# A fused two-layer latent-attention kernel: averages in two PSUM banks a step apart, apart-row scores and small values by chunk of two batches, GpSimd's ones and products later and a step apart

## The chip, the cores and the metric

The kernel runs on one core of one Trainium2 chip. The metric is device time in microseconds of one launch; the profile is one such execution. The engines are TensorE (PE, with its weight loads shown as PEld), VectorE (DVE), ScalarE (ACT), GpSimd (POOL) and the queue of SyncE (SP), which issues the DMAs. Each engine works through its own instructions in order.

## The reference

16 batches of 64 latents of width 128 pass through two layers. Each layer is cross attention to a context, then a scan over the latents, then a feed-forward part, each on the layer-normed latents and added to them:

```python
x = x + _L0_xattn_ref(ctx_1024, _layernorm(x), ...)     # 16 heads of 64
x = x + _L0_attn_ref(_layernorm(x), ...)                # selective scan
x = x + _L0_ffn_ref(_layernorm(x), ...)                 # small attention, then 8 experts, top 2, and a shared one
x = x + _L1_xattn_ref(ctx_1024, _layernorm(x), mask, ...)
x = x + _L1_attn_ref(_layernorm(x), ...)                # convolution and a scan in blocks
x = x + _L1_ffn_ref(_layernorm(x), ...)                 # weights and inputs rounded to 4 bits
...
# cross attention, both layers (layer 1 with a mask over the context rows):
kv_input = concatenate([layernorm(ctx), layernorm(latents)])   # 1601 + 64 rows
logits = einsum('bhld,bhsd->bhls', q * scale, k * scale)
out = einsum('bhls,bhsd->bhld', softmax(logits), v) @ Wo
```

Everything is float32.

## The kernel before

**Tiling.** The cross attention is done for groups: a group is a layer, a batch and half of its 16 heads, 8 heads x 64 latents = 512 columns, so there are 64 groups. The query weights are folded with the key weights (`wqk`) and the value weights with the output weights (`wvo`), so that keys and values are the normed context itself. `kv` holds a batch's 13 tiles of 128 rows (12 context tiles `G`, and a last one with 64 context rows and the 64 latent rows), with a column of ones as the 129th for the softmax's denominator; `kvT` is its transpose. The 1601st context row doesn't fit and is handled apart: its scores `se` (`apart_scores`, L403 to L418) are small matmuls of the latents `xnT` with a folded vector per head (`ge`), and its contribution comes in as `xeb` times `ee` when the averages are read.

**Steps.** `run` counts steps `n`; 13 steps (`NT`) are a group's score tiles. `step` issues at each `n`:

- `scores` (L643): one matmul of 512 columns (L656) into one of three PSUM tiles `s`; DVE keeps the running maximum over the tiles, `R` (L664 masked, layer 1; L666 layer 0), and ACT copies the tile to `st` in SBUF (L669, L671). `st` tiles hold two score tiles each, and there are 11 of them.
- `average` (L709), `LAG` = 21 steps behind the scores: four matmuls of 129 columns (L719), `st` as weights and `kv` as the moving side, accumulated over the 13 tiles in `av`, one PSUM tile that spans two banks. At a group's first tile nothing is issued; the first two tiles come together a step later. So with i = n mod 13 the averages of step i = 7 are the last of a group, step 8 has none, step 9 has eight matmuls.
- `gather` (L721): after the last average DVE reads `av` with four operations (L728) into `aq`. Only then may the next group's averages start, since there is one `av`.
- after a group's scores: `maximum` (transposes `tm`, L680, and the row's maximum, with `se`), `spread` (`mb`, L698), and at every second step `weigh`: DVE subtracts the maximum (L706), ACT takes the exponential (L707).
- after its averages: `denominator` (reciprocal L767, division on GpSimd L768), `turn` (transposes `at`, L779), and for the second half of every second batch `output` (L791), at fixed offsets of steps.

The preparation of a batch runs beside it: `context_load` (L468) at 48 steps ahead issues on SP the DMAs of `kv` (L486, L487 from the context in layer 0; L489, L490 from the stored normed copy in layer 1), and on GpSimd a memset of the ones column (L472). Three `kv` tiles rotate, so both wait for the last average of three batches earlier. `context` (L576), a generator that gives one portion of work per step, norms it (layer 0: first reduction L606 on DVE, statistics on ACT, L612, square root on GpSimd, L135), transposes it, stores it and calls `with_latents` (L563), which multiplies `kv` by the norm's weight on GpSimd (four operations, L570) and adds the latents' columns and rows. The scan and feed-forward parts of finished batches (`scan0`, `moe`, `scan1`, `ffn`) are generators too, from which a budget takes portions between the steps. In `moe` the values `mv` (L943) of the small attention are one matmul per batch.

**Order.** The Tile framework's scheduler orders each engine's instructions from these issues; `behind` adds order-only dependencies that keep a portion of side work behind the main instruction just issued. So the order on an engine may differ from the order of issue in small ways.

```python
LAG = 21
...
self.pss = pool("pss", 3, space=PSUM)      # s
self.psa = pool("psa", 1, space=PSUM)      # av
self.pst = pool("pst", 3, space=PSUM)      # everything else, "tp"
...
grp["av"] = self.psa.tile([P, 2, NQ], F32, tag="av", name=f"av{g}")
```

Of the kernel before, what the change touches and what calls it, by code (L numbers as in the profile page):

```python
# [79 lines left out]
class Kernel:  # L80
# [236 lines left out]
    def raw_pair(self, lay, l, r, g, queue):  # L317


        if lay == 0:  # L320
            t = self.at.tile([P, 2, NQ], F32, tag="st2", name=f"raw{l}{g}", bufs=11)
            pair = [t[:, i, :2 * D].rearrange("p (m d) -> p m d", m=2) for i in range(2)]
        else:
            pair = [self.at.tile([P, 2, D], F32, tag="raw", name=f"raw{n}{g}", bufs=3) for n in (l, r)]
        for t, n in zip(pair, (l, r)):
            queue.dma_start(out=t, in_=self.a[f"L{lay}{n}"].rearrange("(m p) d -> p m d", p=P)[:, 2 * g:2 * g + 2, :])
        return pair
# [75 lines left out]
    def apart_scores(self, lay, b):  # L403

        nc = self.nc
        bl = b % BG
        xnT = self.lat_of[lay, b // BG][0][:, bl * L:(bl + 1) * L]
        t = self.tp(f"se{lay}_{b}")
        ge = self.ge[:, b, :].rearrange("p (n i) -> p i n", i=2)
        for i in range(2):  # L410
            nc.tensor.matmul(t[i * L:(i + 1) * L, :H // 2], xnT, ge[:, i, :], start=True, stop=True)
        se = self.sm([P, H // 2], "se")
        if lay == 0:
            nc.vector.tensor_copy(se, t[:, :H // 2])
        else:
            nc.vector.tensor_scalar(se, t[:, :H // 2], self.mex[:, b:b + 1], None, ALU.add)
        self.se_of[lay, b] = se
        yield 0.3  # L418
# [49 lines left out]
    def context_load(self, lay, b):  # L468
        nc = self.nc
        kv = self.at.tile([P, G + 1, D + 1], F32, tag="kv", name=f"kv{lay}_{b}", bufs=3)  # L470
        kvT = self.at.tile([P, SK + L], F32, tag="kvT", name=f"kvT{lay}_{b}", bufs=2)
        nc.gpsimd.memset(kv[:, :, D:], 1.0)  # L472
        if lay == 0:
            ctxd = self.a["ctx"]
            tiles = ctxd[b, :P * G, :].rearrange("(p g) d -> p g d", g=G)
            nc.gpsimd.memset(kv[64:P, G, :D], 0.0)
            if b == 0:

                self.raw_kv = [self.at.tile([P, 2, NQ], F32, tag="st2", name=f"rkv{j}", bufs=11).rearrange("p i (g d) -> p (i g) d", d=D) for j in range(2)]
                for lo in range(0, G, 4):  # L480
                    nc.sync.dma_start(out=self.raw_kv[lo // 8][:, lo % 8:lo % 8 + 4, :], in_=tiles[:, lo:lo + 4, :])
                    if lo == 0:
                        self.raw0.append(self.raw_pair(0, "WqT", "WkT", 1, nc.sync))
                nc.sync.dma_start(out=self.raw_kv[1][:REM, G - 8, :], in_=ctxd[b, P * G:SK, :])
            else:
                nc.sync.dma_start(out=kv[:, :G, :D], in_=tiles)  # L486
                nc.sync.dma_start(out=kv[:REM, G, :D], in_=ctxd[b, P * G:SK, :])  # L487
        else:
            nc.sync.dma_start(out=kv[:, :, :D], in_=self.xh[b])  # L489
            nc.sync.dma_start(out=kvT[:, :SK], in_=self.xhT[b])  # L490
        self.kv_of[lay, b] = (kv, kvT)

    def first_context(self):
# [28 lines left out]
        def turned(lo, hi):  # L522
# [7 lines left out]
            raw = self.at.tile([P, 2, NQ], F32, tag="st2", name=f"xt{lo}", bufs=11)[:, 0, :w]  # L530
# [29 lines left out]
        self.with_latents(0, 0)  # L560
        yield 0.0

    def with_latents(self, lay, b):  # L563
# [3 lines left out]
        kv, kvT = self.kv_of[lay, b]  # L567

        for lo, hi in ((0, 4), (4, 7), (7, 10), (10, G + 1)):
            nc.gpsimd.tensor_tensor(kv[:, lo:hi, :D], kv[:, lo:hi, :D], self.row(self.vec[:, w1, :], [P, hi - lo, D]), ALU.mult)  # L570
        xnT, xn = self.lat_of[lay, b // BG]
        bl = b % BG
        nc.scalar.activation(kvT[:, SK:], xnT[:, bl * L:(bl + 1) * L], AF.Identity, bias=self.nvcol[:, b1:b1 + 1])
        nc.sync.dma_start(out=kv[REM:, G, :D], in_=xn[(bl % 2) * L:(bl % 2 + 1) * L, bl // 2, :])

    def context(self, lay, b):  # L576
# [26 lines left out]
        elif lay == 0:  # L603
            nmean, rstd, v, off = (self.sm([P, n], f"c{x}") for x in ("mean", "rstd", "var", "off"))
# [35 lines left out]
        self.with_latents(lay, b)  # L640
        yield 1.0

    def scores(self, g, i):  # L643
# [6 lines left out]
        if i % 2 == 0:  # L650
            n = min(2, NT - i)
            grp["st"].append(self.at.tile([P, n, NQ], F32, tag=f"st{n}", name=f"st{g}_{i // 2}", bufs=11 if n == 2 else 2))
# [56 lines left out]
    def average(self, g, i):  # L709
# [4 lines left out]
        if i == 0:  # L714
            grp["av"] = self.psa.tile([P, 2, NQ], F32, tag="av", name=f"av{g}")
        for k in range(4):
            o = grp["av"][:, k // 2, k % 2 * (D + 1):(k % 2 + 1) * (D + 1)]
            st = grp["st"][i // 2][:, i % 2, k * P:(k + 1) * P]
            nc.tensor.matmul(o, st, self.kv_of[lay, b][0][:, i, :], start=(i == 0 and k % 2 == 0), stop=(i == NT - 1 and k % 2 == 1))  # L719

    def gather(self, g):  # L721

        nc, grp = self.nc, self.groups[g]
        aq = grp["aq"] = self.at.tile([P, 4, D + 1], F32, tag="aq", name=f"aq{g}", bufs=2)
        xeb = self.xeb_of[grp["key"][:2]]
        for k in range(4):
            o = grp["av"][:, k // 2, k % 2 * (D + 1):(k % 2 + 1) * (D + 1)]
            nc.vector.scalar_tensor_tensor(aq[:, k, :], xeb, grp["ee"][:, k:k + 1], o, ALU.mult, ALU.add)  # L728
        for k in ("st", "R", "av", "mb"):
            grp.pop(k)  # L730

    def finish(self, g):
# [6 lines left out]
        xeb, av = self.xeb_of[lay, b], grp["av"]  # L739
        blocks = av[:, :, :2 * (D + 1)].rearrange("p k (j d) -> p k j d", j=2)  # L740
        four = lambda v: v.rearrange("p (k j) -> p k j", k=2)
        den, rd = self.sm([P, 4], "den"), self.sm([P, 4], "rd")
        nc.vector.tensor_tensor(four(den), blocks[:, :, :, D], four(grp["ee"]), ALU.add)
        nc.vector.reciprocal(rd, den)
        turned = []
        for k in range(4):
            nc.vector.scalar_tensor_tensor(aq[:, k, :D], xeb[:, :D], grp["ee"][:, k:k + 1], blocks[:, k // 2, k % 2, :D], ALU.mult, ALU.add)
# [13 lines left out]
        for k in ("st", "R", "av", "mb"):  # L761
            grp.pop(k)
# [147 lines left out]
    def moe(self, gr):  # L910
        nc, tc, a = self.nc, self.tc, self.a
        X = self.X[:, gr * CG:(gr + 1) * CG, :]
        with tc.tile_pool(name="mo1", bufs=1) as one, tc.tile_pool(name="mo2", bufs=2) as work:
# [28 lines left out]
            for b in range(BG):  # L942
                nc.tensor.matmul(t[b % 2 * L:(b % 2 + 1) * L, b // 2 * 32:(b // 2 + 1) * 32], xT[:, b * L:(b + 1) * L], fWkvT[:, 32:], start=True, stop=True)  # L943
# [475 lines left out]
    def run(self, out):  # L1419
# [6 lines left out]
        done = lambda lay, b: start(lay, b) + LAG + 9  # L1426
# [12 lines left out]
        for lay in range(2):  # L1439
# [14 lines left out]
            for b in range(NB):  # L1454
                if lay or b:
                    prep.append((max(start(lay, b) - (28 if lay == 0 else 12), 3), 2 if lay == 0 else 1, self.context(lay, b)))
                prep.append((start(lay, b) - 2 if lay or b else 12, 1, self.apart_scores(lay, b)))
# [10 lines left out]
        self.summed, self.upto_sums = False, upto_sums  # L1468
# [93 lines left out]
    def step(self, n, ng):  # L1562
# [4 lines left out]
        ga, ia = divmod(n - LAG, NT)  # L1567
        if 0 <= ga < ng and ia:
            if ia == 1:
                self.average(ga, 0)  # L1570
            self.average(ga, ia)
            if ia == NT - 1:
                if ga == ng - 1:
                    self.upto_sums()
                    self.finish(ga)
                else:
                    self.gather(ga)
# [15 lines left out]
        if 0 <= d < ng:  # L1593
# [3 lines left out]
            with self.behind():  # L1597
                if o == 0:
                    self.denominator(d)
                elif o == 4:  # L1600
                    self.turn(d)
                if o == 7 and b % 2 and half:
                    self.output(lay, b // 2)
                elif o == 9 and d == ng - 2:
# [58 lines left out]
```

## Time and profile before

| what | value |
|---|---|
| median of 3 runs | 1988.09 us (1985.63 to 1988.84) |
| the profiled execution, its own time | 1984.66 us |
| its span, first to last instruction | 1983.0 us |
| granted TensorE clock over the span | 0.999 |
| PE busy | 1938.7 us |
| DVE busy | 1557.6 us |
| ACT busy | 1380.2 us |
| POOL busy | 516.1 us |

Busy time is the time in which at least one instruction of an engine was running. In the profile a line such as L719 is a line of the kernel's file; "x6656" is the number of records, and one float32 matmul of the program shows as two records. In the groups, the number after the bar is busy time in us, then the mean of one record in ns, then the idle time of the engine just before these instructions and what ended it. In the waits, a row is: engine and instruction that waited, what it waited for, us in total, how many times, the longest. In the timeline a row is: start in us, length, engine, line, instruction, how many merged.

### The profile page before, as it was taken

Reading aid. Unit: us, or ns where it says so; the run is one execution under the profiler, and the core shown is the slowest. Engines: PE = TensorE matmul, PEld = TensorE weight load, DVE = VectorE, ACT = ScalarE, POOL = GpSimd, SP = SyncE. Lnnn points to the kernel's source line nnn. Section 1 sums busy time; section 2 is a strip of 40 time slices with the busy share of each in tenths; the row PEclk is TensorE's granted clock in tenths of the full one; section 3 lists DMA queues with packets and bytes.
Section 4 is the critical chain, followed back from the end, with each engine's and each line's share of the span. In section 5 each row is a group of like instructions: output and inputs, shape, how many; then the busy total and the mean of one; then the engine's idle time right before and its main releaser. Section 6 shows DMA issues by size and latency. Waiting matters only on the chain. (4 is left out here: it accounts for less than half of the span.)

```text
span 1983.0 us, 32835 instructions
## 1 busy us (share of the span) xinstructions
PE 1938.7 (98%) x12083; PEld 1476.6 (74%) x12083; DVE 1557.6 (79%) x2976; ACT 1380.2 (70%) x2642; POOL 516.1 (26%) x579
## 2 busy tenths in 40 slices
PE   8999999999999999999999999999999999999998
PEld 5777777677777767768777777777778777787787
DVE  6977667977868787775998778898786878777885
ACT  5787778887768888656766667776665656765561
POOL 5211122543113552121542202442110121101000
PEclk9999999999999999999999999999999999999999
DMA  6121112322122121221221112221120211101000
GB/s 178 51 68 43 46 53 77 92 58 70 29 81 85 60 82 53 66 79 45 68 82 53 41 32 71 70 58 53 49 67 2 58 37 37 42 17 37 24 1 22
DMA packets 144110, 110.82 MB, mean 56 GB/s; under 512 B 13762, under 2 KB 130254, under 8 KB 143950
## 3 DMA queue, kind: packets, MB, share of 16 engines
q1 hardware_dynamic: 143406, 108.46, 18.8%
q8 instruction: 96, 1.57, 0.3%
q14 instruction: 64, 0.52, 0.1%
q10 hardware_dynamic: 544, 0.26, 0.0%
HBM read 80.23 MB, written 27.41 MB: 54 GB/s over the span
## 5 line engine op out<-in xcount | busy, mean ns | idle before, releaser
L719 PEld LDWEIGHTS av<-kv,st 128*128 128x128 f32 x6656 | 853.3, 192 | 324.0 <-issue 305.9
L719 PE MATMUL av<-kv,st 128*128 128x129 f32 x6656 | 866.3, 275 | 3.2 <-DVE aq L728 2.5
L656 PE MATMUL s<-qT,kvT 128*128 128x512 f32 x1664 | 850.6, 599 | 16.0 <-ACT st L671 8.7
L707 ACT ACTIVATE st<-st 128x1024 f32<-128x1024 f32 (+1 forms) x448 | 445.6, 999 | 113.2 <-DVE st L706 110.4
L706 DVE TENSOR_TENSOR st<-st,mb 128x1024 f32<-128x1024 f32 (+1 forms) x448 | 505.2, 1133 | 19.8 <-PE mb L698 19.8
L669 ACT ACTIVATE st<-s,mcol 128x512 f32<-128x512 f32 x416 | 283.8, 683 | 217.3 <-DVE R L664 173.5
L671 ACT COPY st<-s 128x512 f32<-128x512 f32 x416 | 240.5, 580 | 132.5 <-DVE R L666 101.1
L656 PEld LDWEIGHTS s<-qT,kvT 128*128 128x128 f32 x1664 | 258.7, 191 | 77.9 <-ACT st L671 28.3
L664 DVE SCALAR_TENSOR_TENSOR R<-s,mcol,R 128x512 f32<-128x512 f32 x352 | 261.8, 744 | 42.3 <-PE s L656 40.8
L666 DVE TENSOR_TENSOR R<-s,R 128x512 f32<-128x512 f32 x352 | 240.5, 683 | 44.4 <-PE s L656 43.7
L570 POOL TENSOR_TENSOR kv<-kv,vec 128x384 f32<-128x384 f32 (+1 forms) x128 | 132.2, 1054 | 169.3 <-DMA xh<-kv 63.9
L768 POOL TENSOR_TENSOR aq<-aq,rd 128x512 f32<-128x512 f32 x63 | 71.4, 1134 | 354.6 <-DVE rd L767 349.3
L872 POOL TENSOR_TENSOR db<-sc_u,bb 128x512 f32<-128x512 f32 x64 | 84.6, 1324 | 141.0 <-DVE h L883 86.1
L889 POOL TENSOR_TENSOR sc_y<-sc_y,h 128x512 f32<-128x512 f32 x60 | 86.0, 1434 | 98.1 <-DVE h L888 81.5
L883 DVE TENSOR_TENSOR_SCAN h<-da,db 128x512 f32<-128x512 f32 x64 | 82.3, 1286 | 0.0
L621 ACT ACTIVATE kv<-kv,coff,crstd 128x128 f32<-128x128 f32 x182 | 76.3, 492 | 4.1 <-POOL coff L618 4.1
L612 ACT ACTIVATE scr<-kv,cmean 128x128 f32<-128x128 f32 x182 | 73.0, 401 | 3.0
L666 DVE TENSOR_TENSOR R<-s,st 128x512 f32<-128x512 f32 x32 | 22.0, 687 | 66.7 <-PE s L656 54.6
L135 POOL TENSOR_TENSOR crstd<-cvar,neghalf 128x13 f32<-128x13 f32 x14 | 34.2, 2440 | 152.0 <-DVE cvar L616 152.0
L728 DVE SCALAR_TENSOR_TENSOR aq<-xeb,ee,av 128x129 f32<-128x129 f32 x252 | 72.0, 341 | 1.0 <-PE av L719 0.8
L455 PE MATMUL q<-xnT,wqk 128*128 128x128 f32 x512 | 69.5, 278 | 0.3
L455 PEld LDWEIGHTS q<-xnT,wqk 128*128 128x128 f32 x512 | 63.1, 192 | 8.5 <-issue 3.0
(409 smaller groups left out, 1927.8 us busy)
## 6 DMA issues: line engine op xcount, KB each, us to landing
bb<-bcd SPq DMA_DIRECT2D x64, 256.0 KB, 4.6
xh<-kv SPq DMA_DIRECT2D x16, 832.0 KB, 4.8
kv<-xh SPq DMA_DIRECT2D x16, 832.0 KB, 5.6
kvT<-xhT SPq DMA_DIRECT2D x16, 800.0 KB, 4.6
xhT<-kvT SPq DMA_DIRECT2D x15, 800.0 KB, 3.4
kv<-in_ctx_dram SPq DMA_DIRECT2D x15, 768.0 KB, 5.5
ew<-in_e1T_dram SPq DMA_DIRECT2D x36, 64.0 KB, 1.8
ew<-in_e3T_dram SPq DMA_DIRECT2D x36, 64.0 KB, 1.9
```

Source lines behind the costliest of these rows:

```text
L455: nc.tensor.matmul(t[:, k * P:(k + 1) * P], self.wqk[:, g * 4 + k, :], xnT, start=True, stop=True)
L570: nc.gpsimd.tensor_tensor(kv[:, lo:hi, :D], kv[:, lo:hi, :D], self.row(self.vec[:, w1, :], [P, hi - lo, D]), ALU.mult)
L656: mm = nc.tensor.matmul(s, self.kv_of[lay, b][1][:, i * P:(i + 1) * P], q, start=True, stop=True)
L664: mx = nc.vector.scalar_tensor_tensor(R, s, mc, last, ALU.add, ALU.max)
L666: mx = nc.vector.tensor_tensor(R, s, last, ALU.max)
L669: ev = nc.scalar.activation(st, s, AF.Identity, bias=mc)
L671: ev = nc.scalar.copy(st, s)
L706: nc.vector.tensor_tensor(st, st, self.row(mb, [P, n, NQ]), ALU.subtract)
L707: nc.scalar.activation(st, st, AF.Exp)
L719: nc.tensor.matmul(o, st, self.kv_of[lay, b][0][:, i, :], start=(i == 0 and k % 2 == 0), stop=(i == NT - 1 and k % 2 == 1))
L872: nc.gpsimd.tensor_tensor(db, u, self.row(bb[:, 0, s % 2, :], both), ALU.mult)
L889: nc.gpsimd.tensor_tensor(y, y, h, ALU.add)
```

## The change

- **Averages.** `av` becomes two PSUM tiles of one bank each, `av0` and `av1`, with two of the four blocks each. `step` issues the first half's matmuls 21 steps behind the scores and the second half's 22 steps behind; at the very last tile both come in one step. Each half is read by two DVE operations after its own last average. `denominator`, `turn` and `output` come one step later, as does the start of the scan parts (`done`). There are 12 `st` tiles of two in place of 11.
- **Apart-row scores.** One matmul for a chunk of two batches (128 latents, 2 x 16 columns), called for every second batch, in place of two matmuls of 64 latents and 8 columns for each batch. Half of its output is not used (each batch's latents with the other batch's vector). DVE copies four blocks of 64 x 8 per chunk to the two `se` tiles, and in layer 1 adds the mask with an operation for each.
- **Small values.** `mv` in `moe` is a matmul per chunk of 128 latents in place of one per batch of 64.
- **GpSimd.** The memset of the ones, except for the first two batches of layer 0, moves from `context_load` to `with_latents`, after the latents' columns on ACT; the zeroing of the last tile's lower half in layer 0 moves from `context_load` to the beginning of `context`. The four products with the norm's weight are issued one step apart instead of all in one step.

```diff
-    def apart_scores(self, lay, b):
+    def apart_scores(self, lay, c):
...
-        xnT = self.lat_of[lay, b // BG][0][:, bl * L:(bl + 1) * L]
-        t = self.tp(f"se{lay}_{b}")
-        ge = self.ge[:, b, :].rearrange("p (n i) -> p i n", i=2)
-        for i in range(2):
-            nc.tensor.matmul(t[i * L:(i + 1) * L, :H // 2], xnT, ge[:, i, :], start=True, stop=True)
-        se = self.sm([P, H // 2], "se")
-        if lay == 0:
-            nc.vector.tensor_copy(se, t[:, :H // 2])
-        else:
-            nc.vector.tensor_scalar(se, t[:, :H // 2], self.mex[:, b:b + 1], None, ALU.add)
-        self.se_of[lay, b] = se
+        xnT = self.lat_of[lay, c // CG][0][:, (c % CG) * P:(c % CG + 1) * P]
+        t = self.tp(f"se{lay}_{c}")
+        nc.tensor.matmul(t[:, :2 * H], xnT, self.ge[:, 2 * c:2 * c + 2, :].rearrange("p b h -> p (b h)"), start=True, stop=True)
+        for j in range(2):
+            se = self.sm([P, H // 2], "se")
+            mine = t[j * L:(j + 1) * L, j * H:(j + 1) * H].rearrange("p (n i) -> p i n", i=2)
+            for i in range(2):
+                nc.vector.tensor_copy(se[i * L:(i + 1) * L, :], mine[:, i])
+            if lay:
+                nc.vector.tensor_scalar(se, se, self.mex[:, 2 * c + j:2 * c + j + 1], None, ALU.add)
+            self.se_of[lay, 2 * c + j] = se
...
# context_load
-        nc.gpsimd.memset(kv[:, :, D:], 1.0)
+        if lay == 0 and b < 2:
+            nc.gpsimd.memset(kv[:, :, D:], 1.0)
+            nc.gpsimd.memset(kv[64:P, G, :D], 0.0)
...
-            nc.gpsimd.memset(kv[64:P, G, :D], 0.0)
...
# with_latents, now a generator
-        for lo, hi in ((0, 4), (4, 7), (7, 10), (10, G + 1)):
-            nc.gpsimd.tensor_tensor(kv[:, lo:hi, :D], kv[:, lo:hi, :D], self.row(self.vec[:, w1, :], [P, hi - lo, D]), ALU.mult)
         xnT, xn = self.lat_of[lay, b // BG]
         bl = b % BG
         nc.scalar.activation(kvT[:, SK:], xnT[:, bl * L:(bl + 1) * L], AF.Identity, bias=self.nvcol[:, b1:b1 + 1])
+        if lay or b > 1:
+            nc.gpsimd.memset(kv[:, :, D:], 1.0)
+
+        for lo, hi in ((0, 4), (4, 7), (7, 10), (10, G + 1)):
+            nc.gpsimd.tensor_tensor(kv[:, lo:hi, :D], kv[:, lo:hi, :D], self.row(self.vec[:, w1, :], [P, hi - lo, D]), ALU.mult)
+            yield 0.6
         nc.sync.dma_start(out=kv[REM:, G, :D], in_=xn[(bl % 2) * L:(bl % 2 + 1) * L, bl // 2, :])
...
# context, layer 0, before the first reduction
+            nc.gpsimd.memset(kv[64:P, G, :D], 0.0)
...
-    def average(self, g, i):
+    def average(self, g, i, j):
...
         if i == 0:
-            grp["av"] = self.psa.tile([P, 2, NQ], F32, tag="av", name=f"av{g}")
-        for k in range(4):
-            o = grp["av"][:, k // 2, k % 2 * (D + 1):(k % 2 + 1) * (D + 1)]
-            st = grp["st"][i // 2][:, i % 2, k * P:(k + 1) * P]
-            nc.tensor.matmul(o, st, self.kv_of[lay, b][0][:, i, :], start=(i == 0 and k % 2 == 0), stop=(i == NT - 1 and k % 2 == 1))
+            t = self.psa.tile([P, NQ], F32, tag=f"av{j}", name=f"av{g}_{j}")
+            grp["av", j] = t[:, :2 * (D + 1)].rearrange("p (k d) -> p k d", k=2)
+        for k in range(2):
+            st = grp["st"][i // 2][:, i % 2, (2 * j + k) * P:(2 * j + k + 1) * P]
+            nc.tensor.matmul(grp["av", j][:, k, :], st, self.kv_of[lay, b][0][:, i, :], start=(i == 0 and k == 0), stop=(i == NT - 1 and k == 1))
...
# moe
-            for b in range(BG):
-                nc.tensor.matmul(t[b % 2 * L:(b % 2 + 1) * L, b // 2 * 32:(b // 2 + 1) * 32], xT[:, b * L:(b + 1) * L], fWkvT[:, 32:], start=True, stop=True)
+            for c in range(CG):
+                nc.tensor.matmul(t[:, c * 32:(c + 1) * 32], xT[:, c * P:(c + 1) * P], fWkvT[:, 32:], start=True, stop=True)
...
# run
-        done = lambda lay, b: start(lay, b) + LAG + 9
+        done = lambda lay, b: start(lay, b) + LAG + 10
...
# step
-        ga, ia = divmod(n - LAG, NT)
-        if 0 <= ga < ng and ia:
+        for j in range(2):
+            ga, ia = divmod(n - LAG - j, NT)
+            if not 0 <= ga < ng or not ia:
+                continue
+            end = ga == ng - 1 and ia == NT - 1
+            if j and end:
+                continue
             if ia == 1:
-                self.average(ga, 0)
-            self.average(ga, ia)
-            if ia == NT - 1:
-                if ga == ng - 1:
-                    self.upto_sums()
-                    self.finish(ga)
-                else:
-                    self.gather(ga)
+                self.average(ga, 0, j)
+            self.average(ga, ia, j)
+            if end:
+                self.late_half = ga
+            elif ia == NT - 1:
+                self.gather(ga, j)
+        if self.late_half is not None:
+            self.average(self.late_half, NT - 1, 1)
+            self.upto_sums()
+            self.finish(self.late_half)
+            self.late_half = None
...
-                if o == 0:
+                if o == 1:
                     self.denominator(d)
-                elif o == 4:
+                elif o == 5:
                     self.turn(d)
-                if o == 7 and b % 2 and half:
+                if o == 8 and b % 2 and half:
                     self.output(lay, b // 2)
```

## The prediction

> **What bounds the kernel now.** I read the page first (busy shares and groups), then the waits of PE, then PE's timeline at two kinds of place, and last the waits of POOL and of the context's first reduction on DVE.
>
> The page:
>
> ```profile
> PE 1938.7 (98%) x12083; PEld 1476.6 (74%) x12083; DVE 1557.6 (79%) x2976; ACT 1380.2 (70%) x2642; POOL 516.1 (26%) x579
> ...
> L719 PE MATMUL av<-kv,st 128*128 128x129 f32 x6656 | 866.3, 275 | 3.2 <-DVE aq L728 2.5
> L656 PE MATMUL s<-qT,kvT 128*128 128x512 f32 x1664 | 850.6, 599 | 16.0 <-ACT st L671 8.7
> ```
>
> PE is the bound. The program has 3328 average matmuls and the profile 6656 records, so each matmul is two records. A change can gain here in two ways only: fewer or cheaper PE instructions, or fewer stalls of PE. The page's idle time, 1983.0 - 1938.7 = 44 us, is too small a measure of stalls: a matmul's modelled end reaches into the gap after it. I therefore use the distance from start to start. PE's timeline, a group end of layer 1:
>
> ```profile
> 1214.02 1.02 PE L656 MATMUL s<-qT,kvT 128*128 128x512 f32 x2
> 1214.88 1.05 PE L719 MATMUL av<-kv,st 128*128 128x129 f32 x8
> 1215.77 1.88 PE L656 MATMUL s<-qT,kvT 128*128 128x512 f32 x4
> 1219.51 1.12 PE L656 MATMUL s<-qT,kvT 128*128 128x512 f32 x2 [1.86 <-ACT st L669]
> 1220.47 2.84 PE L719 MATMUL av<-kv,st 128*128 128x129 f32 x24
> ```
>
> One score tile takes 0.86 us (1214.02 to 1214.88), one tile's averages 0.89 us (to 1215.77); a step is 1.75 us and 832 of them are 1456 us of the span. But at a group's end three score tiles stand in a row (x4 and x2, no averages between), because step 8 has no averages and step 9's are behind a scheduler that put tile 10 first. The third should start at 1215.77 + 2 x 0.86 = 1217.49 and starts at 1219.51: 2.02 us lost, for a PSUM tile that ACT had not yet read. In the instruction order 31 of 64 ends have tiles 8, 9, 10 in a row, 30 others 8 and 9. Measured start to start over all group ends: tile 9 is late 15 times, tile 10 15 times, the new group's first average 14 times (it waits for the four readings of the one `av` tile, L728), in sum 25.7 us. A middle tile (0 to 8, 12) is late by about 1 us in all 64 groups together.
>
> The second place, the apart-row scores:
>
> ```profile
> 508.45 1.05 PE L719 MATMUL av<-kv,st 128*128 128x129 f32 x8
> 509.43 0.29 PE L411 MATMUL se<-ge,xnT 128*64 128x8 f32 x4
> 509.65 1.13 PE L656 MATMUL s<-qT,kvT 128*128 128x512 f32 x2
> 510.62 1.05 PE L719 MATMUL av<-kv,st 128*128 128x129 f32 x8
> ```
>
> From av to s is 1.20 us where 0.89 is usual, from s to av 0.97 where 0.86 is usual: 0.31 + 0.11 = 0.42 us for four tiny records. The pattern is the same at nearly all 32 calls.
>
> **The change, part by part.** (a) Apart scores by chunk. Removed: 32 calls x 0.415 us (the trace's ns at this place) = 13.3 us. Added: 16 calls of one 128x32 matmul, two records, on the whole array. The nearest row is the router's, small but untiled:
>
> ```profile
> 1408.93 1.05 PE L719 MATMUL av<-kv,st 128*128 128x129 f32 x8
> 1409.82 0.51 PE L1055 MATMUL router<-w_WrT,mo_xT 128*128 128x8 f32 x4
> 1410.19 1.10 PE L656 MATMUL s<-qT,kvT 128*128 128x512 f32 x2
> 1411.13 1.05 PE L719 MATMUL av<-kv,st 128*128 128x129 f32 x8
> ```
>
> Here four records cost (1410.19 - 1409.82) + (0.94 - 0.86) = 0.45 us, 0.112 each. Two are 0.224 us, 16 calls 3.6 us. Gain 9.7 us. Here a rule speaks for the old form: the Trainium skill, "TensorEngine Tiling (Array Packing)", section Overview, gives narrow operands up to 2x when the array is split, two tiles side by side. The trace shows that overlap (the second record of a pair starts 7 ns after the first), and by this rule alone a call would be two pairs of 0.112, 7.2 us in all, and the gain only 3.6. But the measured call has 93 ns ahead of the tiny records and some 310 to the next start. The page has the reason too (section Tiling Modes, key properties: changing the mode drains TensorE), without a price; the row has it. I take 9.7, and 3.6 as the low end. Beside it DVE gets 64 copies and 16 additions in place of 32 operations: copies of 8 columns have a row at 156 ns (L414), the old masked form 215 (L416), so 64 x 0.156 + 16 x 0.2 = 13 us in place of 5.9, +7 us on an engine with 425 us free. It is hidden as long as three score tiles in PSUM bridge it: one call is 0.6 us in layer 0 and about 0.85 in layer 1, against 1.75 - 1.35 = 0.4 us free on DVE in each step (0.74 for the maximum and half of 1.21 for the weighing), so the backlog is gone in one or two steps. I charge 1 us in all, 0 to 5.
>
> (b) Small values by chunk: 4 calls of 8 tiled records, about 0.55 us each without their wait, become 4 untiled records at 0.112, 0.45. Gain 0.4 us; 0.45 and 0.87 us of waits for ACT ahead of two of them stay.
>
> (c) Averages in two halves a step apart. The number of matmuls and records is the same. The order of instructions of the changed kernel reads, between tiles 7 and 12: tile 8, 2 averages, tile 9, 4, tile 10, 6, tile 11, 4; 51 of the 64 ends have exactly this and only two still have 9 and 10 side by side. So tile 9 starts half of 0.89 = 0.45 us later by work instead of waiting, and tile 10 another 0.89, 1.34 together. I let each stall of the trace shrink by that (tile 9 by 0.45, tile 10 of a row of three by 1.34, the first average by 0.9, as its two readings now have two score tiles and a half step of averages in front of them), and count 0.10 us for a refill where something is left: of 25.7 us, 20.0 go. The big ones remain in part (the 2.02 us above keeps 0.7: DVE and ACT are also held by scan work there). Against it: new small stalls at two boundaries in place of one, 3 us by the rate of middle tiles (two or three tiles at 1 us per 64). Net 17 us; at most 25.7, at least 6 if DVE and ACT are the ones that can't keep up and the wait only moves. Alternating between two banks is no new cost: the old order already changed banks after every second matmul, and x8 still took 0.89.
>
> Moved with it by one step: the division (L767, L768), the turn, the output. PE then has turn at step 0 instead of after tile 12, and the output beside `mb` at step 3; these are PE work, no wait: the division has four steps (7 us) as before for 1.13 us on POOL. The `st` tiles live a step longer, and one buffer more (two steps) covers it; ACT's waits for a free one (6.4 + 1.3 us) can only shrink. The kv tile comes free a step later, see the rival. In the tail one reading fewer stands before the last group's averages (0.5 us gained), one `den` operation of 0.16 us is added: +0.3.
>
> (d) GpSimd.
>
> ```profile
> POOL kv L472 <- PE av L719: 184.7, 22, 30.8
> ...
> PE at L779 <- POOL aq L768: 2.4, 1, 2.4
> ```
>
> The memset of ones waited 184.7 us at the head of POOL's queue; moved, it waits for nothing. But PE waited for POOL only once, 2.4 us. DVE's waits for POOL's square roots (L135) are 16 us in all, the longest 2.4, and DVE has the slack. Gain 0 to 3, I take 0.5. The products, a step apart, end three steps later, still more than 20 steps ahead of the first average that reads them; behind them on SP only the latents' rows. The zeroing of the last tile's lower half now stands directly before DVE's second reduction of the same tile; POOL must be less than a step late there. I charge 1 us, 0 to 4.
>
> Sum: 9.7 + 0.4 + 17 + 0.3 + 0.5 - 1 - 1 = 25.9, say 26 us. The profiled run took 1984.66 us (span 1983.0), so it becomes 1958.7; the median of three is 1988.09, 3.4 above the profiled run, so 1962.
>
> **The rivals.** *The stalls only move* (chance 0.2). DVE at 79% and ACT at 70% are the reason that a PSUM tile is late; if their backlog at a group end is the whole matter, (c) gives 6 instead of 17, (a) its 9.7 less 3 for the bunched copies: 12 us, 1976. For it: ACT's 173.5 us of waits for DVE's maximum. Against: DVE itself waits 170 us for PE's scores, so it is ahead on average.
>
> *A late context, slower than before* (0.07). The kv tile is free only after the second half's last average, 1.75 us later; its load is waiting for that, and DVE's reduction heads DVE's queue:
>
> ```profile
> DVE cmean L606 <- DMA kv<-in_ctx_dram: 10.4, 9, 2.1
> ```
>
> With 1.75 us more at 13 contexts of layer 0 that is up to 10.4 + 13 x 1.75 = 33 us of DVE held, the maximum behind it, the PSUM tile behind that. If PE took all of it, 33 - 26 = 7 us slower, 1995; it decides from about 26 of the 33 us reaching PE, 2 us per context. Against: none of the nine waits of before (up to 2.1 us) is followed by a stall of PE, three tiles last 5 us, and in the new order this reduction stands behind tile 10's maximum in 13 of 14 cases (7 of 14 before), which gives the step back.
>
> *It does not do what it says*, no change (0.05): the scores' gain is eaten by copies and the stalls come back elsewhere. The order of instructions speaks against it.
>
> **How the numbers follow.** My forecast, 0.68: 1962, its own range 1952 to 1970. Best case: 25.7 + 9.7 + 3 = 38 us, 1950. Down the stalls that only move, 1976, with 4 more for the ends of (a) and (d), 1980. The range 1950 to 1980 leaves out the late context, the no change and a little on the fast side. A measurement of this kernel tells about 0.2%, 4 us, from no change. Faster by more: 0.68 + 0.2 less 0.01; within: 0.05; slower: 0.08.
>
> **What would show it.** Right: no x4 of s at group ends in PE's timeline; `se` 32 records at about 0.22 us a call with s following at once; PE's waits for ACT st and for DVE aq together under 8 us (17.8 before); POOL's wait for av gone. Wrong: new waits of s for ACT or DVE at tiles 11 to 2, where the copies and the reductions stand; cmean's wait for its DMA at 20 us or more; PE busy falling by less than 10 us.

## The result and the profile after

| kernel | median (5 runs each) | ratio to before, 95% interval |
|---|---|---|
| before | 1987.88 us (1985.63 to 1988.84) | |
| after | 1976.48 us (1974.50 to 1977.40) | 0.9943 (0.9931 to 0.9954) |

The changed kernel is 11.4 us faster, 0.6%. The forecast was 26 us: the sign was right and the size less than half. The time is that of the rival "the stalls only move", 1976. The profiled execution took 1976.84 us (span 1975.1), 7.8 less than the profiled one of before. The 33 runs of before beside e1 to e4 took 1989.5 us in the mean where the granted clock was 0.997 and 1986.3 where it was 0.999, so a difference of 2 us between a few runs may be the clock.

The page after, engines and the three groups that matter (busy us, mean ns, idle before and what ended it):

```profile
PE 1931.2 (98%) x11971; PEld 1478.7 (75%) x11971; DVE 1584.3 (80%) x3025; ACT 1385.2 (70%) x2642; POOL 510.4 (26%) x579
...
L725 PE MATMUL av<-kv,st 128*128 128x129 f32 x6656 | 882.2, 275 | 4.1 <-DVE aq L734 4.0
L662 PE MATMUL s<-qT,kvT 128*128 128x512 f32 x1664 | 857.7, 598 | 9.1 <-ACT st L677 6.6
...
L889 DVE TENSOR_TENSOR_SCAN h<-da,db 128x512 f32<-128x512 f32 x64 | 91.4, 1429 | 0.5 <-ACT da L877 0.5
```

112 PE records are gone and PE's busy time fell by 7.5 us. DVE's rose by 26.7 us, to 1584.3, where the forecast had +7. The readings of the apart scores (L414, L416) went from 5.9 to 21.7 us. Another 9.1 us is not new work: the scan, which the change does not touch, took 1286 ns a record before and takes 1429. Before:

```profile
L883 DVE TENSOR_TENSOR_SCAN h<-da,db 128x512 f32<-128x512 f32 x64 | 82.3, 1286 | 0.0
```

PE's waits before, and after (total, times, longest):

```profile
PE s L656 <- ACT st L671: 8.7, 15, 1.2
PE s L656 <- ACT st L669: 6.6, 10, 1.9
PE av L719 <- DVE aq L728: 2.5, 6, 0.9
```

```profile
PE s L662 <- ACT st L677: 6.6, 11, 1.4
PE av L725 <- DVE aq L734: 4.0, 5, 1.3
...
PE mb L704 <- DVE tm L695: 2.5, 4, 1.4
PE mb L704 <- DVE m L693: 2.0, 2, 1.5
PE s L662 <- ACT st L675: 1.6, 4, 0.8
```

The waits for ACT's `st` and DVE's `aq` together are 6.6 + 4.0 + 1.6 = 12.2 us (17.8 before; forecast under 8), and the two rows of `mb`, the spread maximum, are new. PE's timeline at the group end that the prediction showed:

```profile
1209.49 1.02 PE L662 MATMUL s<-qT,kvT 128*128 128x512 f32 x2
1210.35 0.61 PE L725 MATMUL av<-kv,st 128*128 128x129 f32 x4
1210.80 1.02 PE L662 MATMUL s<-qT,kvT 128*128 128x512 f32 x2
1211.66 1.05 PE L725 MATMUL av<-kv,st 128*128 128x129 f32 x8
1212.55 1.02 PE L662 MATMUL s<-qT,kvT 128*128 128x512 f32 x2
1213.41 1.50 PE L725 MATMUL av<-kv,st 128*128 128x129 f32 x12
1214.75 1.02 PE L662 MATMUL s<-qT,kvT 128*128 128x512 f32 x2
```

Here the mechanism is as forecast: averages in records of 4, 8, 12 between the score tiles, each score tile 0.86 us and each start following on the last; the 2.02 us lost there before are gone. Over the whole trace two or more score tiles stand in a row at 6 places, before at 58. Another place, inside the scan of layer 0 (PE and DVE):

```profile
354.44 0.59 DVE L734 SCALAR_TENSOR_TENSOR aq<-xeb,ee,av 128x129 f32<-128x129 f32 x2
...
354.95 0.68 DVE L672 TENSOR_TENSOR R<-s,R 128x512 f32<-128x512 f32 x1
...
355.08 1.16 PE L725 MATMUL av<-kv,st 128*128 128x129 f32 x8 [1.34 <-DVE aq L734]
```

PE's averages wait 1.34 us for the readings of their half, which DVE began only at 354.44. DVE was late here, not PE's order. Start to start over the whole trace (distances longer than usual by more than 40 ns, summed, in us):

| where PE is late | before | after |
|---|---|---|
| score tiles 9 and 10 | 19.6 | 5.4 |
| apart scores with the refill behind them | 14.6 | 3.3 |
| first averages of a group | 8.3 | 10.2 |
| `mb` | 0 | 6.7 |
| tiles 3 to 8 | 4.7 | 6.8 |
| tiles 11 to 2 (3.1 of before is that refill) | 8.2 | 8.1 |
| router and expert portions (`me`, `gr`) | 3.3 | 5.6 |

The first two rows give 25.5 us, nearly what the prediction wanted of them. The others take 13 back, or 16 if the refill is counted once, and the span fell by 7.9. (The sums don't close exactly: lateness under 40 ns isn't in them.)

### The profile page after: what moved, and what is told of

Its sections match the earlier page's. It is cut to its first block, busy times and chain, and to the rows that moved or that the text cites. A ratio compares the mean times of both kernels' runs of the same rounds, so it can differ in the third digit from the quotient of the medians.

```text
span 1975.1 us, 32602 instructions
## 1 busy us (share of the span) xinstructions
PE 1931.2 (98%) x11971; PEld 1478.7 (75%) x11971; DVE 1584.3 (80%) x3025; ACT 1385.2 (70%) x2642; POOL 510.4 (26%) x579
## 5 line engine op out<-in xcount | busy, mean ns | idle before, releaser
L725 PEld LDWEIGHTS av<-kv,st 128*128 128x128 f32 x6656 | 870.0, 192 | 375.7 <-issue 356.3
L725 PE MATMUL av<-kv,st 128*128 128x129 f32 x6656 | 882.2, 275 | 4.1 <-DVE aq L734 4.0
L712 DVE TENSOR_TENSOR st<-st,mb 128x1024 f32<-128x1024 f32 (+1 forms) x448 | 503.5, 1134 | 17.9 <-PE mb L704 17.8
L662 PEld LDWEIGHTS s<-qT,kvT 128*128 128x128 f32 x1664 | 254.4, 191 | 24.7 <-ACT st L677 11.5
L895 POOL TENSOR_TENSOR sc_y<-sc_y,h 128x512 f32<-128x512 f32 x60 | 80.9, 1349 | 117.4 <-DVE h L894 100.9
L889 DVE TENSOR_TENSOR_SCAN h<-da,db 128x512 f32<-128x512 f32 x64 | 91.4, 1429 | 0.5 <-ACT da L877 0.5
L734 DVE SCALAR_TENSOR_TENSOR aq<-xeb,ee,av 128x129 f32<-128x129 f32 x252 | 76.2, 341 | 0.0
```

The source lines that it names most:

```text
L662: mm = nc.tensor.matmul(s, self.kv_of[lay, b][1][:, i * P:(i + 1) * P], q, start=True, stop=True)
L712: nc.vector.tensor_tensor(st, st, self.row(mb, [P, n, NQ]), ALU.subtract)
L725: nc.tensor.matmul(grp["av", j][:, k, :], st, self.kv_of[lay, b][0][:, i, :], start=(i == 0 and k == 0), stop=(i == NT - 1 and k == 1))
L889: nc.vector.tensor_tensor_scan(flat(h), flat(da), flat(db), 0.0, ALU.mult, ALU.add)
```

## The experiments

**The parts one by one.** My theory was that the gain at the group ends is real but DVE, already full in the scan's stretches, takes it back; against it, that one part costs time by itself. Three kernels carry one part each.

Halves alone (e1): before, with `average`, `gather`, `finish` by half, the offsets and the 12th `st` tile.

```diff
-            grp["av"] = self.psa.tile([P, 2, NQ], F32, tag="av", name=f"av{g}")
...
+            t = self.psa.tile([P, NQ], F32, tag=f"av{j}", name=f"av{g}_{j}")
```

> The kernel before with the averages' halves alone: two banks, the second half a step later, 12 score-tile buffers, division, turn and output a step later. Theory A (the halves do what was forecast, and the lost time is DVE's new work with the scores and its waits for GpSimd): the 14 us of late tiles 9 and 10 go and nothing new comes, about 1973 us (-13 to -17). Theory B (DVE and ACT can't keep up at group ends, so the late tiles only move): 1980 to 1984 us (-4 to -8), with new stalls of score tiles or of the spread maximum elsewhere, and DVE's busy time as before (1558 us).

1977.28 us, 0.9947 (0.9934 to 0.9959): -10.9 us, between the two theories. The scan's mean is already 1448 ns here.

Scores and small values alone (e2):

```diff
-            nc.tensor.matmul(t[i * L:(i + 1) * L, :H // 2], xnT, ge[:, i, :], start=True, stop=True)
...
+        nc.tensor.matmul(t[:, :2 * H], xnT, self.ge[:, 2 * c:2 * c + 2, :].rearrange("p b h -> p (b h)"), start=True, stop=True)
```

> The kernel before with the apart-row scores and the small values by chunk alone. PE saves about 10 us in either theory. Theory A: DVE's busy time rises by 15 us or more, the masked addition of layer 1 (SBUF to SBUF) takes 0.5 to 0.7 us in place of 0.2 as it ends with a GpSimd instruction, and 3 to 6 us come back as stalls: 1982 to 1985 us. Theory B: the work on DVE is hidden, 1978 us (-10).

1987.31 us, 0.9999 (0.9990 to 1.0007): nothing, and less than either theory gave. PE's block of apart scores did shrink, 11.5 to 4.6 us without the refill, but tiles 9 and 10 grew from 19.6 to 23.2, the first averages from 8.3 to 11.2, tiles 3 to 8 from 4.7 to 7.9. Its group of score matmuls, and PE at the end shown in the prediction:

```profile
L656 PE MATMUL s<-qT,kvT 128*128 128x512 f32 x1664 | 852.6, 600 | 21.0 <-ACT st L671 12.2 <-ACT st L669 7.9 <-ACT kvT L529 0.5
```

```profile
1219.66 1.88 PE L656 MATMUL s<-qT,kvT 128*128 128x512 f32 x4
1223.40 1.12 PE L656 MATMUL s<-qT,kvT 128*128 128x512 f32 x2 [1.86 <-ACT st L669]
```

The idle time before `s` is 21.0 us where it was 16.0. A part of what PE saves it waits out at the next group end, whose stall of 1.86 us stands as before. This profiled execution took 1989.71 us, 2.4 more than the median, but those of e5, e9 and e14, at their medians, say the same: PE's waits of `s` for ACT's `st`, 15.3 us before, are 21.5 us in e5 below, and 18.7 in e14 where e9 has 14.5. That is 4 to 6 of some 10 us; the rest went at other tiles and was not followed.

GpSimd's part alone (e3): the memsets and the spaced products.

```diff
-        nc.gpsimd.memset(kv[:, :, D:], 1.0)
...
+        if lay or b > 1:
+            nc.gpsimd.memset(kv[:, :, D:], 1.0)
...
+            yield 0.6
```

> The kernel before with GpSimd's ones, zeroing and products moved alone. Theory A: the products now lie beside DVE's scan and are waited for, DVE's scan goes from 1.29 to about 1.4 us a piece, 0 to 4 us slower than before (1988 to 1992). Theory B: nothing, 1986 to 1989 us, and the scan's mean as before.

1986.61 us, 0.9992 (0.9986 to 0.9999): -1.6 us, theory B, and of this 1 us may be the clock (0.9985 in the mean, 0.9978 before); the scan stays at 1285 ns. The three parts give 10.9 + 0.9 + 1.6 = 13.4, near the 11.4 of all together. So no part is seen to spoil another; (c) and (a) are each smaller than forecast.

**The new readings of DVE.** In the changed kernel the mask is added in SBUF. DVE's rows after:

```profile
L416 DVE TENSOR_SCALAR se<-se,mex x16: 217/742/1207, 951.8 to 1790.3; 128x8 f32<-128x8 f32 x16
```

and before, reading PSUM:

```profile
L416 DVE TENSOR_SCALAR se<-se,mex x16: 192/216/226, 958.1 to 1853.6; 128x8 f32<-128x8 f32 x16
```

The stretch of after:

```profile
1296.98 1.18 POOL L578 TENSOR_TENSOR kv<-kv,vec 128x512 f32<-128x512 f32 x1 [0.83 <-DVE se L414]
1297.07 1.13 DVE L416 TENSOR_SCALAR se<-se,mex 128x8 f32<-128x8 f32 x1
```

The addition of eight columns takes 217 ns at least and 1207 at most (ns: least, middle, most); before it was 192 to 226. Here it began 0.09 us after a product on GpSimd and ended with it, at 1298.20 against 1298.16. In 13 of the 16 it took 348 ns or more, and an instruction of GpSimd ends 23 to 33 ns ahead of its end; the other three took 217 to 221. So it is held, not working. e4 adds the mask while reading PSUM, in four operations of 64 x 8:

```diff
-                nc.vector.tensor_copy(se[i * L:(i + 1) * L, :], mine[:, i])
-            if lay:
-                nc.vector.tensor_scalar(se, se, self.mex[:, 2 * c + j:2 * c + j + 1], None, ALU.add)
+                if lay:
+                    nc.vector.tensor_scalar(se[i * L:(i + 1) * L, :], mine[:, i], self.mex[j * L:(j + 1) * L, 2 * c + j:2 * c + j + 1], None, ALU.add)
```

> The changed kernel, with layer 1's mask added while the scores are read from PSUM (four additions per chunk in place of four copies and two additions in SBUF). Theory A: the addition takes about 0.2 us each and no longer ends with a GpSimd instruction, DVE's busy time falls by 8 to 11 us, and the waits of PE for the maximum in layer 1 (about 3 us) and some late score tiles go: 1971 to 1974 us. Theory B: DVE's small work is hidden, 1976 us as the changed kernel.

1973.45 us, 0.9927 (0.9913 to 0.9940), 3 us under the changed kernel by medians (the intervals still overlap a little). DVE's busy time fell by 6.0 us where 8 to 11 were expected, and PE's waits of `mb` for DVE stayed, 4.5 and 4.2 us; where the 3 us came from is not shown.

```profile
L415 DVE TENSOR_SCALAR se<-se,mex x32: 207/225/233, 952.5 to 1787.1; 64x8 f32<-64x8 f32 x32
```

None is held. Next PE's side and DVE's side of the scores were told apart: e5 has the new matmul with the old number of readings, e6 the old matmuls with the new readings, e7 is the changed kernel with the old number.

```diff
# e5 and e7
+            mine = t[:, j * H:j * H + H // 2]
# e6
+        for i in range(2):
+            nc.vector.tensor_copy(se[i * L:(i + 1) * L, :], t[i * L:(i + 1) * L, :H // 2])
```

> The kernel before with the apart-row scores and small values by chunk on PE, but DVE reads each batch with one operation as before (it takes the chunk output's first 8 columns of the batch, so the scores are not the right ones: the selection by head is left out). It has PE's new work and DVE's old work. Theory A (DVE's new readings ate PE's gain): 1978 to 1980 us (-8 to -10). Theory C (the time that PE no longer spends on the scores is waited out at the next group end, since there a PSUM tile is late anyway and PE is not what limits): 1985 to 1988 us (0 to -3), with tiles 9 and 10 and the first averages later than the 28 us of before.

> The kernel before with its own tiled scores on PE, but with DVE's new readings (two copies per batch, in layer 1 then an addition in SBUF): PE's old work and DVE's new work. Theory A: slower by what was lost, 1996 to 1998 us (+8 to +10). Theory C: 1988 to 1991 us (0 to +3).

> The changed kernel with one DVE reading per batch instead of two copies and the masked addition (selection by head left out, as in the run on the kernel before). Theory A: the waits of PE for the maximum and for late tiles shrink, 1968 to 1971 us. Theory C: 1973 to 1975 us, no better than with the mask added from PSUM (1973.5).

| kernel | median, us | ratio (interval) | against before, us |
|---|---|---|---|
| e5, PE's side alone | 1985.43 | 0.9989 (0.9981 to 0.9997) | -2.1 |
| e6, DVE's side alone | 1991.74 | 1.0025 (1.0015 to 1.0035) | +4.2 |
| e7, changed, old readings | 1971.27 | 0.9918 (0.9905 to 0.9931) | -16.3 |

e5 and e6 came out as theory C or next to it, e7 as theory A or next to it. The readings, which I had charged with 1 us, cost 4 to 5 (e6; e7 against the changed kernel). PE's side, even with no new reading, is worth 2 us on the kernel before, but about 6 on top of the halves (e7 is 1971.27, e1 1977.28, of which GpSimd's part may be 1.6).

**Is the held scan the cost?** In the changed kernel 17 of the 64 scans begin inside a GpSimd addition to `sc_y` and are held by it (5 before): they end about 1.08 us after that addition does, where a free scan takes 1.215 us in all. e8 is e4 with the division, turn and output back at their old offsets, which should move the scans back.

```diff
-                if o == 1:
+                if o == 0:
                     self.denominator(d)
-                elif o == 5:
+                elif o == 4:
                     self.turn(d)
```

> The changed kernel with the mask added from PSUM, and with the division, the turn, the output and the scan parts' start at their old steps (one step earlier than in the changed kernel). In this order of instructions the scan on DVE stands less often directly behind the multiplication that starts GpSimd's addition. Theory D (the halves lost part of their gain because DVE's scan is now held by GpSimd's additions: 17 scans of 64 began inside one, 5 before): the scan's mean goes back from 1.43 to 1.30 us, DVE's busy time falls by 8 us, and the time is 2 to 5 us under the 1973.5 of the version with the mask from PSUM alone. Rival: the scan's mean falls but the time stays within 1 us, as DVE has slack there.

The scan's mean fell, 1435 to 1334 ns, and DVE's busy time from 1578.3 to 1567.8, yet the kernel took 1979.83 us, 0.9959 (0.9946 to 0.9972), 6 us more than e4. Both the theory and its rival missed. But e8 is no test of the scan alone: against e4's trace 989 of PE's 11971 records and 586 of DVE's 3009 stand at other places of their engine's order, and the score tiles 9 and 10 are later again by some 3 us. So it shows that shorter scans are not enough, not that held ones cost nothing.

**Relieving DVE in the scan's stretches.** The windows' sums over the four layer-0 scan stretches (331 to 455, 626 to 748, 937 to 1057, 1219 to 1335 us: 482 us together; they are those of after, and before's begin up to 6 us later), of before and of after:

```profile
sum 482.00, PE 472.19 PEld 353.37 DVE 425.05 ACT 377.23 POOL 226.59; mean PE 118.05 PEld 88.34 DVE 106.26 ACT 94.31 POOL 56.65
```

```profile
sum 482.00, PE 465.64 PEld 348.61 DVE 437.41 ACT 375.06 POOL 222.96; mean PE 116.41 PEld 87.15 DVE 109.35 ACT 93.76 POOL 55.74
```

DVE is 88% busy there before (425.05 / 482) and 91% after, while PE falls to 97%. Of DVE's 425 us of slack over the span only 57 lay here, 35 of them waits for PE's scores. So DVE is ahead here at most moments too, but 57 us over the 275 steps of 1.75 us are 0.21 us a step to make up for a late one. e9 and e10 are the kernels before and after without the 60 multiplications `h * cc` of the scan, which in the changed kernel take 45.4 us of DVE.

```diff
                 else:
-                    nc.vector.tensor_tensor(h, h, cc, ALU.mult)
                     nc.gpsimd.tensor_tensor(y, y, h, ALU.add)
```

> The kernel before with less work on DVE in layer 0's scans: 60 multiplications of 0.77 us (the states with the output vector) are left out, 46 us of DVE, all in the stretches where DVE has its backlog. The base for the next run. If DVE binds PE in those stretches, 6 to 12 us under the kernel before (1976 to 1982): of 14 us of stalls in the two scan stretches most go. If PE alone binds, within 3 us of 1988.

> The changed kernel with the same 60 multiplications left out. What counts is its distance to the run before it. Theory C (in the scan stretches of layer 0 DVE is late whatever PE's order is, and the late tiles there only became late first averages; with DVE relieved the change brings what it brings elsewhere): 14 to 20 us under it, and the stalls of groups 11 to 14 and 22 to 25 (18 us in the changed kernel) fall under 8. Rival (the rest of the forecast gain is lost all over the kernel, at DVE's new readings and by the reordering): 9 to 12 us under it, as without this.

e9: 1984.80 us, 0.9982 (0.9973 to 0.9991), -3.4, not the 6 to 12 of a DVE that binds: in the kernel before, DVE's load costs little. e10: 1959.94 us, 0.9863 (0.9847 to 0.9880), 16.5 under the changed kernel. With DVE relieved the change is worth 24.9 us, more than the 14 to 20 expected here and almost the 26 of the forecast (1 us of it may be the clock, 0.9985 in the mean against 0.9977). e10's waits at the places of before:

```profile
PE s L662 <- ACT st L677: 8.9, 11, 1.5
...
PE av L725 <- DVE aq L734: 0.6, 2, 0.3
...
PE mb L704 <- ACT kvT L642: 0.5, 1, 0.5
```

`av` waits for DVE 0.6 us in place of 4.0, and `mb` waits for DVE no more. One part of the expectation failed: the stalls of groups 11 to 14 and 22 to 25, the first two scan stretches, should have fallen below 8 us and fell from 18.3 to 13.6 only; more went in the other two. PE's lateness inside and outside the four stretches, each kernel's own (start to start as above, over the median distance behind the same kind of record; the stretches of 3.4 us in which the profile has half the granted clock, one in after and none in the other two, are left out):

| us late | before | after | e10 |
|---|---|---|---|
| in the four scan stretches | 21.5 | 27.5 | 15.8 |
| elsewhere | 69.5 | 54.9 | 52.2 |

The change took 15 us outside the stretches and lost 6 inside; relieving DVE took 12 inside and 3 outside. PE's order is no rival here: that of e10 differs from the changed kernel's in 2 of 11971 records. On DVE 65 records and on ACT 60 stand elsewhere. What the relief consists of is not told apart: in e10 no scan begins inside an addition to `sc_y` any more, and the scan's mean is 1273 ns.

e13 and e14 do the same for one part each, halves alone and scores alone.

```diff
# e1 and e2, both with
-                    nc.vector.tensor_tensor(h, h, cc, ALU.mult)
```

> The halves alone, with the 60 multiplications on DVE in layer 0's scans left out; to be held against the kernel before with the same left out (1984.8). Theory E (forecast right on PE, wrong on DVE's cover for both parts): 14 to 18 us under it, 1967 to 1971. Rival (the halves bring 11 us wherever DVE stands and relief helps only the scores): 1973 to 1975.

> The scores and small values by chunk alone, with the same multiplications left out; against 1984.8. Theory E' (without the halves, the 10 us that PE saves are waited out at the group ends, relieved or not): within 4 us, 1981 to 1986. Rival (relief alone makes the saving visible): 1975 to 1978.

e13: 1965.29 us, 0.9886 (0.9869 to 0.9902), 19.5 under e9: the 17 forecast for the halves are there (2 of the 19.5 may be the clock, 0.9990 in the mean against 0.9977). e14: 1983.87 us, 0.9982 (0.9973 to 0.9991), 0.9 under e9, as theory E' had it: without the halves the scores give nothing clear even with DVE relieved. e10 is 5.4 under e13: on top of the halves they do.

**Better versions.** e11 is e4 with half of the readings of `se` on ACT.

```diff
+                if i and lay:
+                    nc.scalar.activation(to, mine[:, i], AF.Identity, bias=mx)
+                elif i:
+                    nc.scalar.copy(to, mine[:, i])
```

> The changed kernel with the mask added from PSUM, and half of the readings of the chunk's scores on ACT instead of DVE (two of four per chunk). DVE's work for the scores is then 32 operations as before. If DVE's readings cost what the runs with one reading showed (5 us in the changed kernel), 1971 to 1973 us; ACT has to fit in 32 short operations, and if that holds up its copies of score tiles as much, 1974 to 1976 us.

1975.18 us, 0.9931 (0.9918 to 0.9943): not better than e4, and the intervals overlap. It lies in the second range of the expectation, but not for the reason given there: PE's waits of `s` for ACT's `st` are 7.6 us, 8.3 in e4. e12 is e4 with the 60 multiplications on GpSimd, everything computed.

```diff
-                    nc.vector.tensor_tensor(h, h, cc, ALU.mult)
+                    nc.gpsimd.tensor_tensor(h, h, cc, ALU.mult)
```

> The changed kernel with the mask added from PSUM, and the 60 multiplications of the scan's states with the output vector on GpSimd instead of DVE; everything is computed. DVE loses 46 us, GpSimd gets about 60 x 1.4 = 84 us. If DVE's load in the scan stretches is what the changed kernel lacks, and GpSimd keeps up, 1960 to 1967 us. If GpSimd's longer chain now holds DVE's scans (each up to a GpSimd operation of 1.4 us, 60 of them) or is late for the next state, 1972 to 1980 us.

1962.17 us (1961.11 to 1963.01), 0.9880 (0.9862 to 0.9898): 23.7 us faster than before, the best here. Its multiplications, and its sum over the same four stretches:

```profile
L895 POOL TENSOR_TENSOR h<-h,bb 128x512 f32<-128x512 f32 x60 | 76.5, 1274 | 111.2 <-DVE h L890 104.5 <-DVE cmean L616 6.5
```

```profile
sum 482.00, PE 472.08 PEld 355.14 DVE 404.11 ACT 377.85 POOL 303.50; mean PE 118.02 PEld 88.78 DVE 101.03 ACT 94.46 POOL 75.88
```

A multiplication takes 1274 ns on GpSimd and 757 on DVE, and it still pays: DVE is at 84% in the stretches (404.11 / 482), PE back at 98%, and GpSimd had the room (63%). Against e4 it gains 11.3 us with 2 of PE's records at another place.

## Why the prediction was right and where it was wrong

- **What bounds the kernel.** PE at 98% was right for the span, and the late tiles 9 and 10 and the block of apart scores were found and mostly removed as the prediction said. The step that failed is "DVE itself waits 170 us for PE's scores, so it is ahead on average": an average says nothing of the moments at which DVE is late, and in the scan stretches, where it is busy 88% before and 91% after, it catches up slowly. There PE became 6 us later instead of earlier, and with DVE relieved the change was worth 24.9 us instead of 11.4. With this sentence the prediction dismissed the rival that came nearest.
- **(a), the price.** By the medians of the calls it was right: 0.415 us a call before and 0.22 after, 9.7 us in all. (The 14.6 - 3.3 = 11.3 us of the table hold a few calls of before that were also waiting.) One reading in it was wrong: the 310 ns are the whole excess from `av` to `s`, 93 ns ahead of the tiny records and 218 from them to the next start. The twofold gain of the Trainium skill, "TensorEngine Tiling (Array Packing)", section Overview, my low end of 3.6, isn't what the isolated tiny tiles gave.
- **(a), the sum.** The 9.7 us were added as if each saved PE microsecond came off the end. Alone they are worth nothing (e2, e14) to 2.1 us (e5), at least in part because a PE that arrives earlier at the next group end waits there longer for the same `st`. On top of the halves they are worth 5 to 6, GpSimd's part included (e10 against e13, e7 against e1). The gains of two parts don't simply add; one opens the way for the other.
- **(a), the cover.** "Hidden as long as three score tiles bridge it", charged 1 of 0 to 5: it cost 4 to 5 (e6, e7). The "0.4 us free on DVE in each step" left out the scan's own work: in the stretches it is 0.21. The addition was sized at 0.2 us from a row that reads PSUM, and measured 713 ns on average when reading and writing SBUF beside GpSimd; this alone is about 3 us of it by e4, not clear of noise. That the rest is DVE's lack of room is argued, not shown.
- **(b), small values.** 0.4 us, in e2 and not told apart.
- **(c), halves.** Tiles 9 and 10 lost what was listed, from 19.6 to 5.4 us. But the first averages grew, 8.3 to 10.2, where they should have shrunk, so that 12.3 us of these stalls went instead of 20. "New small stalls, 3 us" was mis-sized in the changed kernel, where `mb` alone is 6.7; the halves alone have 1.4 there (e1), so this is no cost of the halves by themselves. 17 forecast, 10.9 measured alone, 19.5 with DVE relieved (e13). The lower end of 6 named the cause: DVE can't keep up and the wait moves.
- **The tail**, 0.3 us, wasn't tried by itself.
- **(d).** 0.5 counted as gain for the memset and 1 charged for the zeroing; e3 measured -1.6 (-2.8 to -0.2). "Moved, it waits for nothing" was wrong. POOL's waits after:

```profile
POOL kv L575 <- PE av L725: 113.7, 12, 31.2
...
POOL kv L610 <- PE av L725: 80.6, 9, 17.9
```

  194.3 us at the head of POOL's queue in place of 184.7, for the ones and now for the zeroing too, and PE waits for none of it: its one wait for the division, 2.4 us before, is gone.
- **The rivals.** "The stalls only move" had the time, 1976, with other terms: (c) gave 10.9 instead of 6, and (a) nothing instead of its 9.7 less 3, so that the same number is a coincidence. Its reason, a late DVE, was the right one; it was given 0.2 and deserved more. The late context didn't come: `cmean`'s wait for its DMA is 9.2 us, 10.4 before. The third, no change, is excluded by the interval.
- **The signs.** Right ones: nearly no x4 at group ends (6 places for 58), `se` as forecast. Signs of being wrong that came: 12.2 us where under 8 was asked, PE busy falling by 7.5 where 10 was the least, POOL's wait still there. The new waits stood at `mb` rather than at `s`.

What stays open: why e8 with shorter scans is 6 us slower than e4, what share of the relief in e10 and e12 is fewer operations on DVE and what share is scans no longer held, and how much the moved records on DVE and ACT add. That DVE's load decides is shown by e10, e12 and e13, which take work off DVE and leave PE's order as it was; that it does so in the scan stretches is shown by where PE's lateness fell in e10.

## What to carry to other kernels

Before a saving on the bound engine is added to the sum, look at the stretch in which it falls and ask whether the engines that empty PSUM can catch up there after a late moment; the slack that covers a new small operation is the stretch's, not the span's. Take away the largest stall first: here the smaller saving behind it counted only afterwards. Where DVE is the second bound and GpSimd is idle, a move of work that is dearer on GpSimd can still be the best edit.

## What the hardware did that I had not expected

- A DVE addition of 128 x 8 with source and result in SBUF took 217 ns alone and up to 1207 beside a GpSimd instruction, ending 23 to 33 ns after that one; the same addition from PSUM, in halves of 64 x 8, took 207 to 233 ns at every call (e4). The Trainium skill, "SBUF — State Buffer", section "SBUF: two separate sides", calls the pair of ports that DVE and GpSimd share an exclusive lock for a whole instruction, held by whichever starts first, if the DVE instruction runs in a mode that uses both ports or has two inputs in SBUF. Of the 13 held additions 11 begin after the GpSimd instruction, as this has it; two begin 4 and 28 ns ahead of it and are held too. In which mode the addition ran no run shows.
- A scan that begins inside a GpSimd addition ends about 1.08 us after it, where a free one takes 1.215 us in all. How many are free depends on small shifts: of the 64, 50 were before, 34 after, 48 in e12.
- Four tiny tiled matmul records between full-array ones cost 0.415 us of PE, and two untiled ones 0.22 (medians of the 32 and 16 calls).
